# Cross attention with image prompts: inner products by way of DRAM, and two changes of order

## The chip, the cores and the metric

The kernel runs on one core of a Trainium2 chip. Its engines work side by side: TensorE (PE) multiplies, VectorE (DVE), ScalarE (ACT) and GpSimd (POOL) work on elements, SyncE (SP) issues most transfers. The metric is the device time of one execution in microseconds; every number of times below is in that unit.

## The reference

Eight images (B = 8) of 112 query rows and 320 channels attend to 375 context tokens of 512 features, of which the last 4 are image prompts, with 20 heads of 16 channels. What is computed for each image, cut to what matters:

```python
q   = heads(x @ W_q)                       # 20 heads, 112 x 16
k_t = heads(text @ W_k); v_t = heads(text @ W_v)        # text: 371 tokens
probs_t  = softmax(q k_t^T * scale)        # 112 x 371 for each head
text_out = probs_t @ v_t
k_ip, v_ip = heads(ip @ W_k_ip), heads(ip @ W_v_ip)     # ip: 4 tokens
qsem = l2norm(probs_t @ text)              # 112 x 512 for each head
sem  = qsem @ l2norm(ip)^T
fused    = q k_ip^T * scale + 0.5 * sem
probs_ip = softmax(fused) * spatial_mask
out = (text_out + probs_ip @ v_ip) @ W_out + b_out + x
```

## The kernel before

The kernel never forms `probs_t @ text` (512 wide). For its norm it uses the inner products of the tokens with each other (the Gram matrix, 371 x 371, made once for an image): the norm squared of a row of probabilities p is the sum over p G p. Since G is symmetric, only the part from the diagonal on is kept, doubled, the diagonal blocks halved. The product of p with G, with the prompts, with a column of ones and with the values of the head is one chain of matrix products.

**Steps.** The 20 heads of an image are done in 5 groups of 4 heads, so there are 40 steps, written (image, group). A step has these parts:

- *scores* (L797 to L804): one matrix product for each head, 112 x 375.
- *probabilities* (L806 to L821): the maximum on DVE (L810), the exponential on ACT (L814), and a transfer that writes the head's 112 x 371 probabilities p into the buffer xg (L821, issued by SP). xg has two buffers, used by turns.
- *turning* (`transposed`, L823 to L836): DVE turns xg into xgT, twelve blocks of 32 tokens (BLK = 12), in one instruction of twelve blocks or two of six.
- *placing* (`placed`, L759): POOL copies the head group's 16 value columns from vr into the free columns of u (L763), in three pieces.
- *products* (`product`, L843 to L860): twelve blocks times four heads; the four heads sit on four groups of 32 rows of PE. Weights are xgT, the moving operand is u: 392 columns for block 0, 32 fewer with each block.
- *sums* (`reduced`, L907, on DVE; `value_sums`, L881, on ACT).

**The tile u** holds an image's products and value columns once for each of the four row groups of PE: 128 partitions, four quarters of GW = 792 columns. `gram` (L530) makes the products in the tile ug (128 x 792, one buffer), ACT and POOL double and halve them, and `gram_to_groups` (L551) copies quarter q, that is 32 rows of ug, into all four groups of 32 rows of u: four transfers for a quarter. Quarters are copied at different times: for an odd image in the course of the even image before it, after group 1 (quarter 0), after group 2 (quarter 1), a little later (quarter 2, in `behind`) and after group 3 (quarter 3); for an even image after groups 0, 1, a little later, and 3. Value columns go from the tile vext to DRAM (vd, `values_to_dram`, L692) and from there to vr (`values_to_groups`, L712).

**The order** of PE, SP and DVE is written out by hand (later that of ACT and POOL too), and each engine does its instructions in that order. SP's transfers are issued one after another: one that has to wait holds up all behind it. The steps go in pairs: `pair(n)` does steps n and n + 1 and works on the scores and probabilities of steps n + 2 and n + 3 between their products; `moved` is called after each step's products and issues the copies above; `behind(n)` does the projections, products and turnings between the pairs. The first steps, `alone(0)` and what leads to them, are written out from L1206 on.

One transfer has an unusual count of rows: `load_ctx` loads the last 371 - 11 x 32 = 19 rows of the text with four transfers of 19 rows (L146).

Of the kernel before, what the change touches and what calls it, by code (L numbers as in the profile page):

```python
# [8 lines left out]
F32 = mybir.dt.float32  # L9
# [11 lines left out]
def kernel(  # L21
# [14 lines left out]
    nc = tc.nc  # L36
    P = 128
# [13 lines left out]
    RG = 32  # L51
# [9 lines left out]
    GROUP = 4  # L61
    NG = H // GROUP
    BLK = TP // RG
# [3 lines left out]
    GW = GCOL[NT]  # L67
# [16 lines left out]
    dram = ctx.enter_context(tc.tile_pool(name="dram", bufs=2, space=bass.MemoryType.DRAM))  # L84
# [142 lines left out]
    ug = const.tile([P, GCOL[NT]], F32, tag="ug", name="ug")  # L227
# [191 lines left out]
    st = {}  # L419
# [110 lines left out]
    def gram(b):  # L530
# [3 lines left out]
        for c in range(NT):  # L534
# [13 lines left out]
            doubled(ps, c, c, DEAL[c] if left_out(b, c) else ())  # L548
            yield

    def gram_to_groups(b, blocks, eng=nc.sync):  # L551

        for q in blocks:
            for a in range(GROUP):
                eng.dma_start(
                    st[b]["u"][a * RG : (a + 1) * RG, q * GW : (q + 1) * GW],
                    ug[q * RG : (q + 1) * RG, :],
                )
# [153 lines left out]
    def values_to_groups(b, c0=0, c1=NT):  # L712
        s = st[b]
        w = NG * D
        for a in range(GROUP):
            nc.sync.dma_start(
                s["vr"][a * RG : (a + 1) * RG, c0 * QN : c1 * QN].rearrange(
                    "p j g d -> p j (g d)"
                ),
                s["vd"][c0 * P : c1 * P, a * w : (a + 1) * w].rearrange("(j i) x -> i j x", i=RG),  # L720
            )
# [63 lines left out]
    def scores(b, g, a, early=False, ps=None):  # L785
        s = st[b]
        _, qm, j = queries[b]
        i, r = g // 2, g % 2
        if early and (g + a // 2) % 2:

            ps = ps_qd.tile([P, 512], F32, tag="qd", name=f"ps_s_{b}_{g}_{a}")
        elif ps is None:
            ps = ps_sc.tile([P, 512], F32, tag="sc", name=f"ps_s_{b}_{g}_{a}")
        w = T if b > 0 else TT
        if i == FULL:
            r = a // 2
        nc.tensor.matmul(  # L797
            ps[:S, :w],
            qm[a * RG : (a + 1) * RG, i, r, j * S : (j + 1) * S],
            s["kT"][a * RG : (a + 1) * RG, i, :w],  # L800
            start=True,
            stop=True,
        )
        s["sc", g, a] = ps  # L804

    def probabilities(b, g, a):  # L806
        s = st[b]
        ps = s.pop(("sc", g, a))
        nmx = small.tile([S, 1], F32, tag="nmx", name=f"nmx_{b}_{g}_{a}", bufs=8)
        nc.vector.tensor_reduce(nmx, ps[:S, :TT], AX.X, ALU.max, negate=True)  # L810
        if ("p", g) not in s:
            s["p", g] = work.tile([S, GROUP, TT], F32, tag="p", name=f"p_{b}_{g}", bufs=4)
        p = s["p", g][:, a, :]
        nc.scalar.activation(p, ps[:S, :TT], AF.Exp, bias=nmx)  # L814
        if b > 0:
            nc.scalar.copy(s["ipl"][:, groups[g][a], :], ps[:S, TT:T])  # L816

        xg = x_ring[(b * NG + g) % NX]
        rows = xg[a * RG : a * RG + S // QN, :, :TT]
        eng = nc.scalar if (b, g, a) == (B - 1, NG - 1, GROUP - 1) else nc.sync  # L820
        eng.dma_start(rows, p)  # L821

    def transposed(b, g, j0=0, j1=BLK):  # L823

        xg = x_ring[(b * NG + g) % NX]
        if j1 < j0 + 1:
            return
        if ("xT", g) not in st[b]:
            st[b]["xT", g] = work.tile([P, BLK, P], F32, tag="xgT", name=f"xgT_{b}_{g}")
        xT = st[b]["xT", g]  # L830
        n = BLK // (2 if b == B - 1 or (b, g) == (0, 0) or j1 - j0 < BLK else 1)
        for j in range(j0, j1, n):
            nc.vector.transpose(  # L833
                xT[:, j : j + n].rearrange("p j (k q) -> p q j k", q=QN),
                xg[:, :, j * RG : (j + n) * RG].rearrange("p q (j k) -> p q j k", k=RG),
            )  # L836
# [66 lines left out]
    def reduced(b, g, a0=0, a1=GROUP):  # L903
        s = st[b]
        for a, (h, ps) in list(enumerate(zip(groups[g], s["qd", g])))[a0:a1]:
            p = s["p", g][:, a, :]
            nc.vector.tensor_tensor_reduce(  # L907
                out=p,
                in0=ps[:S, :TT],
                in1=p,  # L910
                scale=1.0,
                scalar=0.0,
                op0=ALU.mult,
                op1=ALU.add,
                accum_out=s["ss"][:, h : h + 1],
            )
        if a1 == GROUP:
            del s["p", g]
# [276 lines left out]
    steps = [(b, g) for b in range(B) for g in range(NG)]  # L1195
# [3 lines left out]
    def run(key, make, pieces=1):  # L1199

        if key not in gens:
            gens[key] = make()
        for _ in range(pieces):
            next(gens[key], None)
# [27 lines left out]
    run(("q", 0), lambda: project_queries(pairs[0]))  # L1232
    run(("k", 0), lambda: keys(0))
    run(("q", 0), None)
    values_to_groups(0)
    for a in range(GROUP):
        scores(0, 0, a, early=True)
        probabilities(0, 0, a)
    run(("q", 0), None)
    run(("k", 0), None)  # L1240
    for a in range(GROUP):
# [63 lines left out]
    inputs = {5: (0, 2), 9: (2, 5), 19: (5, B)}  # L1305

    late = (1, 5)

    def pair(n):

        one, two = steps[n], steps[n + 1]
        b, g = one
        tags = ("mm", "sc") if b % 2 and g == NG - 1 else ("sc", "mm")
        ends = (BLK - 2, BLK - 1)

        products_in(b, g, ("qd",) * GROUP)
        for j in range(BLK - 2):
            product(b, g, j, range(GROUP))
            if j < 2:
                heads = (HIGH, LOW)[j]  # L1320
                coming_scores(n + LEAD, heads, tags[j])
                coming_probabilities(n + LEAD, heads)
            if j == 1:
                if n in late:
                    transposed(*two, 0, BLK // 2)
                transposed(*two, BLK // 2, BLK)
            if j % QN == QN - 1:
                placed(*two, (j // QN,))
        if n == 3:
            load_channels(nc.gpsimd, wo_sb, w_out)  # L1330
            nc.gpsimd.dma_start(sm_sb, smask.unsqueeze(1))
            nc.gpsimd.dma_start(bias_sb, b_out.partition_broadcast(S))
        if n in inputs:
            load_inputs(*inputs[n])
        products_in(*two, (tags[1],) * 2 + (tags[0],) * 2)
        for there, here in ((HIGH, LOW), (LOW, HIGH)):
            product(*two, 0, there)
            for j in ends:
                product(b, g, j, here)
        del st[b]["xT", g]  # L1340
        placed(*two, (NT - 1,))
        moved(b, g)
        if g > 1 and g != 2:
            turned(b + 2)
        if b % 2 and g in (0, NG - 1):
            f(b - 1 - (g == 0))
        if g in (1, 2):
            f(b - 1, 2)
        reduced(b, g)
        if g == 2:  # L1350
            turned(b + 2)
        value_sums(b, g)
        if b % 2 == 0 and b > 0 and g == 1:
            turned_inputs(pairs[b // 2 + 1], 0, FULL)

        b, g = two
        for j in range(1, BLK - 2):
            product(b, g, j, range(GROUP))
            if j == 4:
                coming_scores(n + 1 + LEAD, HIGH, "qd")  # L1360
                coming_probabilities(n + 1 + LEAD, HIGH)
            if j == 7:
                coming_scores(n + 1 + LEAD, LOW, "qd")
                coming_probabilities(n + 1 + LEAD, LOW)
        for heads in (HIGH, LOW):
            for j in ends:
                product(b, g, j, heads)
        del st[b]["xT", g]
        moved(b, g)
        if one in ((b, 2), (b, 3)):  # L1370
            turned(b + 2, 1 + (one == (0, 3)))

    def moved(b, g):

        nb = b + 1
        if b % 2 == 0:
            if g in (1, 2):
                gram_to_groups(nb, (g - 1,))
            if g == 3:
                todo = [lambda: gram_to_groups(nb, (3,)), lambda: values_to_groups(nb)]  # L1380
                for move in reversed(todo) if nb == B - 1 else todo:
                    move()
        else:
            if g in (0, 1):
                gram_to_groups(nb, (g,))
            if g == 2:
                values_to_groups(nb, 0, 2)

    def behind(n):

        b, g = steps[n]
        nb = b + 1
        two = steps[n + 1 : min(n + 3, len(steps) - NG + 1)]

        def tr(i):
            if i < len(two):
                transposed(*two[i], 0, BLK // (1 + i))

        if b % 2 == 0 and g == 0:
            if n == 0:  # L1400
# [107 lines left out]
    for n in range(0, len(steps) - NG, 2):  # L1508
# [4 lines left out]
        b, g = steps[n]  # L1513
# [16 lines left out]
    b = B - 1  # L1530
# [18 lines left out]
    for g in range(NG):  # L1549
# [36 lines left out]
        n = (3, 3, 2, 0)[g]  # L1586
# [71 lines left out]
```

## Time and profile before

| | |
|---|---|
| runs of the kernel | 403.81, 405.58, 406.58; median 405.58 |
| the profiled execution | 403.29, of which the span of the profile is 401.6 |
| granted clock of PE | 0.999 |
| transfers, all queues | 65.86 MB, mean 164 GB/s |
| queue of SP and its like (q1), POOL's queue (q0) | 57.7% and 6.0% of 16 engines' time |
| u<-ug on SP | 120 issues of 99.0 KB, median 590 ns each |
| xg<-p on SP | 159 issues of 162.3 KB |
| SP waiting for ACT ahead of xg<-p (L821 <- ACT ipl) | 56.2 in 44 waits |

How to read it: the page's first part gives the busy time of each engine and its share of the span. The chain that ended last is followed back from the last instruction; an engine's share of it says how much of the span that engine set. A row of waits has the engine, what it wanted to do, whom it waited for, the total, the count and the longest wait. A row of the timeline has the start, the length, the engine, the line, the operation with its output and inputs, the count of merged instructions and in square brackets the idle time before it and what ended it. A row of the windows has, for each engine, busy time and count of instructions in that stretch, then the granted clock, the mean busy share of 16 DMA engines and GB/s.

### The profile page before, as it was taken

How to read it: one execution, taken by the hardware profiler on the slowest of the kernel's cores; microseconds unless marked ns; L12 is line 12 of the kernel's file. 1: busy time of each engine (PE TensorE's matmuls, PEld its weight loads, DVE VectorE, ACT ScalarE, POOL GpSimd, SP SyncE). 2: the span in 40 equal slices, each digit the busy share in tenths (PEclk: the TensorE clock that was granted, in tenths of full speed). 3: DMA queues.
4: the chain of work that ended last, by engine and by line, in shares of the span. 5: the costliest groups of instructions: out<-in, count | busy, mean ns of one | idle time of the engine just before them, and what ended most of it. 6: DMA issues, size and time to landing. Idle time of an engine off the chain costs nothing.

```text
span 401.6 us, 14442 instructions
## 1 busy us (share of the span) xinstructions
PE 396.1 (99%) x5685; PEld 320.2 (80%) x5685; DVE 332.2 (83%) x712; ACT 200.2 (50%) x716; POOL 192.5 (48%) x409
## 2 busy tenths in 40 slices
PE   8999999999999999999999999999999999999996
PEld 8768697888878788878787878877887878887894
DVE  4357689877989988987999898897798988888995
ACT  3255343347434853425652665334843485446864
POOL 8655427052562567051573348432256155804781
PEclk9999999999999999999999999999999999999999
DMA  8979657988577846668657766576846544775321
GB/s 239 217 202 258 155 153 178 210 193 190 149 186 155 202 122 187 155 146 184 169 148 167 193 155 169 160 185 140 191 120 175 130 125 116 197 176 166 108 59 29
DMA packets 58119, 65.86 MB, mean 164 GB/s; under 512 B 20165, under 2 KB 51257, under 8 KB 58052
## 3 DMA queue, kind: packets, MB, share of 16 engines
q1 hardware_dynamic: 54814, 58.23, 57.7%
q0 software_dynamic: 2544, 5.92, 6.0%
q8 instruction: 45, 0.74, 0.9%
q10 hardware_dynamic: 694, 0.80, 0.6%
q14 instruction: 22, 0.18, 0.2%
HBM read 20.22 MB, written 5.22 MB: 63 GB/s over the span
## 4 chain that ended last, share of the span: by engine, by line
PE 96%; DVE 2%; ACT 1%; issue 0%; DVEq 0%
PE ps_qd L854 47%; PE ps_k L571 10%; PE ps_g L541 8%; PE ps_s L797 6%; PE ps_v L613 6%; PE ps_vs L671 6%; PE ps_k L588 3%; PE ps_q L402 3%; PE ps_o L1050 2%; PE ps_g L503 1%; DVE xgT L833 1%; PE ps_w L489 1%; PE ps_c L472 1%; PE ps_q L384 1%; PE ps_a L1041 0%
## 5 line engine op out<-in xcount | busy, mean ns | idle before, releaser
L854 PE MATMUL ps_qd<-u,xgT 32*112 32x72 f32 (+10 forms) x3806 | 216.0, 352 | 0.8 <-DVE xgT L833 0.7
L854 PEld LDWEIGHTS ps_qd<-u,xgT 32*112 32x112 f32 x3806 | 177.5, 172 | 33.5 <-issue 4.2
L833 DVE STREAM_TRANSPOSE xgT<-xg 128x768 f32<-128x768 f32 (+1 forms) x63 | 123.1, 1973 | 4.3 <-DMA xg<-p 4.1
L814 ACT ACTIVATE p<-ps_s,nmx 112x371 f32<-112x371 f32 x160 | 85.5, 585 | 64.9 <-DVE nmx L810 63.9
L810 DVE TENSOR_REDUCE nmx<-ps_s 112x1 f32<-112x371 f32 x160 | 76.8, 534 | 26.2 <-PE ps_s L797 24.6
L763 POOL COPY u<-vr 128x64 f32<-128x64 f32 x120 | 26.9, 237 | 140.8 <-PE ps_qd L854 76.8
L907 DVE CUSTOM_DVE_ANT_0 p<-ps_qd,p 112x371 f32<-112x371 f32 x148 | 71.6, 540 | 10.0 <-ACT pvs L881 7.4
L797 PE MATMUL ps_s<-kT,qm 32*112 32x375 f32 (+1 forms) x320 | 61.0, 485 | 0.0
L881 ACT COPY pvs<-ps_qd 112x21 f32<-112x21 f32 x148 | 21.3, 200 | 52.5 <-DVE ss L907 49.9
L571 PE MATMUL ps_k<-ctxT,wk_sb 128*128 128x371 f32 x128 | 43.4, 482 | 0.0
L571 PEld LDWEIGHTS ps_k<-ctxT,wk_sb 128*128 128x128 f32 x128 | 23.1, 190 | 12.8 <-issue 0.8
L541 PE MATMUL ps_g<-ctxT 128*32 128x119 f32 (+11 forms) x672 | 32.7, 338 | 0.0
L541 PEld LDWEIGHTS ps_g<-ctxT 128*32 128x32 f32 x672 | 27.7, 109 | 6.1 <-issue 1.2
L797 PEld LDWEIGHTS ps_s<-kT,qm 32*112 32x112 f32 x320 | 27.3, 171 | 6.3 <-POOL vext L675 1.1
L460 DVE STREAM_TRANSPOSE ctxT<-ct 128x512 f32<-128x512 f32 x21 | 22.5, 1081 | 6.7 <-DMA ct<-in_ctx_dram 6.7
L816 ACT COPY ipl<-ps_s 112x4 f32<-112x4 f32 x140 | 24.3, 174 | 0.0
L613 PE MATMUL ps_v<-wv_sb,ctxT 128*128 128x320 f32 x80 | 23.6, 442 | 0.0
L613 PEld LDWEIGHTS ps_v<-wv_sb,ctxT 128*128 128x128 f32 x80 | 14.5, 190 | 5.6
L578 ACT COPY kT<-ps_k 128x371 f32<-128x371 f32 x16 | 7.5, 469 | 22.2 <-PE ps_k L571 22.2
L1029 POOL TENSOR_TENSOR vip<-vip,w 112x1280 f32<-112x1280 f32 (+1 forms) x8 | 17.5, 2182 | 0.2 <-DVE w L1023 0.2
L525 POOL TENSOR_TENSOR ug<-ug,half 128x128 f32<-128x128 f32 (+1 forms) x24 | 10.7, 451 | 14.3 <-ACT ug L524 13.0
L520 ACT ACTIVATE ug<-ps_g 128x279 f32<-128x279 f32 (+5 forms) x24 | 8.0, 333 | 17.5 <-PE ps_g L541 10.8
(189 smaller groups left out, 469.1 us busy)
## 6 DMA issues: line engine op xcount, KB each, us to landing
xg<-p SPq DMA_DIRECT2D x159, 162.3 KB
u<-ug SPq DMA_DIRECT2D x120, 99.0 KB
ct<-in_ctx_dram SPq DMA_DIRECT2D x28, 176.0 KB
vip<-vipd SPq DMA_DIRECT2D x7, 560.0 KB
vr<-vd SPq DMA_DIRECT2D x20, 120.0 KB
out_dram<-ob SPq DMA_DIRECT2D x7, 140.0 KB
vd<-vext POOLq DMA_DIRECT2D x12, 80.0 KB, 3.4
vr<-vd SPq DMA_DIRECT2D x12, 80.0 KB
```

The costliest lines, as they stand in the source:

```text
L541: nc.tensor.matmul(ps[p * RG : (p + 1) * RG, s0 : T - t0], ctxT[:, e, t0 + q * RG : t0 + (q + 1) * RG], ctxT[:, e, t0 + s0 : T], start=(e ...
L571: nc.tensor.matmul(ps[:, :TT], wk_sb[:, e, i * P : (i + 1) * P], s["ctxT"][:, e, :TT], start=(e == 0), stop=(e == NE - 1),)
L613: nc.tensor.matmul(ps[:, :C], ctxT[:, e, c * P : (c + 1) * P], wv_sb[:, e, :], start=(e == 0), stop=(e == NE - 1),)
L671: nc.tensor.matmul(ps[:, :CH], a[:, k], t[:, k], start=(k == 0), stop=(k == 1))
L763: nc.gpsimd.tensor_copy(region(b, c)[:, :, UV - c * P :], s["vr"][:, c * QN : (c + 1) * QN, g, :])
L797: nc.tensor.matmul(ps[:S, :w], qm[a * RG : (a + 1) * RG, i, r, j * S : (j + 1) * S], s["kT"][a * RG : (a + 1) * RG, i, :w], start=True, st ...
L810: nc.vector.tensor_reduce(nmx, ps[:S, :TT], AX.X, ALU.max, negate=True)
L814: nc.scalar.activation(p, ps[:S, :TT], AF.Exp, bias=nmx)
L816: nc.scalar.copy(s["ipl"][:, groups[g][a], :], ps[:S, TT:T])
L833: nc.vector.transpose(xT[:, j : j + n].rearrange("p j (k q) -> p q j k", q=QN), xg[:, :, j * RG : (j + n) * RG].rearrange("p q (j k) -> p ...
L854: nc.tensor.matmul(banks[a][:S, j * RG : UW], xT[a * RG : (a + 1) * RG, j, :S], region(b, c)[a * RG : (a + 1) * RG, p, q * RG :], start=(j ...
L907: nc.vector.tensor_tensor_reduce(out=p, in0=ps[:S, :TT], in1=p, scale=1.0, scalar=0.0, op0=ALU.mult, op1=ALU.add, accum_out=s["ss"][:, h : ...
```

## The change

Three things change.

1. For images 1 to 7 the products go by way of DRAM. A new function writes ug (128 x 792) to a DRAM tile ud; `gram_to_groups` then reads a quarter, 32 rows, four times over with one transfer into all 128 partitions of u. The write stands where quarter 0 was copied, and quarters 0 and 1 are read where quarter 1 was copied. Image 0 keeps its sixteen copies.
2. In the first steps, `values_to_groups(0)` is called after the scores and probabilities of step (0,0) and no longer ahead of them.
3. In `pair(1)`, after the sums of step (0,1), three blocks (BLK // 4) of step (0,3) are turned; `behind(2)` turns the other nine. `transposed` takes the whole stretch in one instruction where it doesn't divide.

```diff
+    def gram_to_dram(b):
+
+        st[b]["ud"] = dram.tile([P, GW], F32, tag="ud", name=f"ud_{b}")
+        nc.sync.dma_start(st[b]["ud"], ug)
+
     def gram_to_groups(b, blocks, eng=nc.sync):
 
         for q in blocks:
+            if b > 0:
+                eng.dma_start(
+                    st[b]["u"][:, q * GW : (q + 1) * GW],
+                    st[b]["ud"][q * RG : (q + 1) * RG].unsqueeze(0).to_broadcast([GROUP, RG, GW]),
+                )
+                continue
             for a in range(GROUP):
                 eng.dma_start(
                     st[b]["u"][a * RG : (a + 1) * RG, q * GW : (q + 1) * GW],
...
         n = BLK // (2 if b == B - 1 or (b, g) == (0, 0) or j1 - j0 < BLK else 1)
+        if (j1 - j0) % n:
+            n = j1 - j0
         for j in range(j0, j1, n):
...
-    values_to_groups(0)
     for a in range(GROUP):
         scores(0, 0, a, early=True)
         probabilities(0, 0, a)
+    values_to_groups(0)
...
+    ahead = (1,)
...
         reduced(b, g)
+        if n in ahead:
+            transposed(*steps[n + 2], 0, BLK // 4)
         if g == 2:
             turned(b + 2)
         value_sums(b, g)
...
         nb = b + 1
         if b % 2 == 0:
-            if g in (1, 2):
-                gram_to_groups(nb, (g - 1,))
+            if g == 1:
+                gram_to_dram(nb)
+            if g == 2:
+                gram_to_groups(nb, (0, 1))
             if g == 3:
                 todo = [lambda: gram_to_groups(nb, (3,)), lambda: values_to_groups(nb)]
...
         else:
-            if g in (0, 1):
-                gram_to_groups(nb, (g,))
+            if g == 0:
+                gram_to_dram(nb)
+            if g == 1:
+                gram_to_groups(nb, (0, 1))
             if g == 2:
                 values_to_groups(nb, 0, 2)
...
         def tr(i):
             if i < len(two):
-                transposed(*two[i], 0, BLK // (1 + i))
+                done = BLK // 4 if n - 1 in ahead and i == 0 else 0
+                transposed(*two[i], done, BLK // (1 + i))
```

## The prediction

> **What bounds the kernel now.** I read the page first, then PE's waits, then the windows of the end, then the order of time around the places that the diff touches.
>
> ```profile
> span 401.6 us, 14442 instructions
> PE 396.1 (99%) x5685; PEld 320.2 (80%) x5685; DVE 332.2 (83%) x712; ACT 200.2 (50%) x716; POOL 192.5 (48%) x409
> PE 96%; DVE 2%; ACT 1%; issue 0%; DVEq 0%
> PE ps_w L489 <- DVE waker L213: 1.1, 1, 1.1
> PE ps_qd L854 <- DVE xgT L833: 0.7, 1, 0.7
> 380.00:402.00 22.00, 18.25 (x298) 15.86 (x290) 16.21 (x50) 12.54 (x49) 11.29 (x19) 0.97 0.16 45
> ```
>
> TensorE (PE) is busy for 396.1 of 401.6 us and is 96% of the chain that ended last. Its idle time is 5.5 us: 1.1 at the start, 3.75 in the last 22 us (22.00 less 18.25), and one stall of 0.7 us ahead of the products (L854). The change adds and removes no PE work. So it can gain that stall and little else; but whatever makes a product wait costs its full length. The question is which transfers have slack.
>
> **The three blocks of one turning.**
>
> ```profile
> 48.37 3.58 SPq L821 DMA_DIRECT2D xg<-p  x4
> 54.76 0.99 DVE L810 TENSOR_REDUCE nmx<-ps_s 112x1 f32<-112x371 f32 x2 [1.01 <-PE ps_s L797]
> 59.48 3.01 DVE L833 STREAM_TRANSPOSE xgT<-xg 128x1536 f32<-128x1536 f32 x1
> 60.65 1.30 PE L402 MATMUL ps_q<-xT,wq_sb 128*128 128x224 f32 x6
> 62.64 0.60 PE L854 MATMUL ps_qd<-u,xgT 32*112 32x392 f32 x4 [0.69 <-DVE xgT L833]
> ```
>
> The stall is here: PE ends its projections at 61.95 and waits until the turning of step (0,3), twelve blocks in 3.01 us, is done. The change puts three of the blocks (3.01 / 4 = 0.75 us) ahead of the maxima at 54.76, where VectorE (DVE) sat idle for 1.01 us. They need the probabilities whose last load SP issued by 48.37 + 3.58 = 51.95. With the 1.9 us from issue to use that a row below shows, they are there at 53.9, the blocks end near 54.6, and the maxima don't move. Nine blocks take 2.26 us, so the turning ends near 61.75, ahead of PE: the stall of 0.69 us goes, and PE's own projections are late next. Bounds: a gain of 0.69, or, if the probabilities come late, a loss of at most the 0.75 by which maxima can be pushed. I take -0.7, as the idle time holds the blocks. The new remainder test in the turning only lets pieces of three and nine blocks be cut; it adds one instruction and changes nothing else.
>
> **The first group's order.**
>
> ```profile
> 23.79 1.87 SPq L716 DMA_DIRECT2D vr<-vd  x4
> 24.41 1.95 ACT L814 ACTIVATE p<-ps_s,nmx 112x371 f32<-112x371 f32 x4 [0.52 <-DVE nmx L810]
> 25.76 7.29 SPq L821 DMA_DIRECT2D xg<-p  x8
> 28.00 0.24 POOL L763 COPY u<-vr 128x64 f32<-128x64 f32 x1 [3.27 <-DMA vr<-vd]
> 34.19 1.22 PE L854 MATMUL ps_qd<-u,xgT 32*112 32x392 f32 x10
> ```
>
> The four loads of value columns move behind the first four writes of probabilities in SP's queue: four times 0.91 us (7.29 / 8), that is 3.65 us less the 0.86 by which the first probabilities can start earlier (25.76 to 24.9, the first of ACT's four at 24.41 plus a quarter of 1.95), so the loads end near 30.4 instead of 25.66. POOL's copy followed the last of them by 2.3 us and would run near 32.7, ahead of the products at 34.19 by 1.5 us. What stands behind it on POOL (input loads, constants, the halving of the next products) slips by 4.7 us and has no reader before 40 us. No idle time stands before the products at 34.19, so the earlier turning gains nothing. I take 0. Bounds: 0, and +0.8 if the loads take twice the 2.3 us.
>
> **Inner products by way of DRAM.** Before, each image's products go to the four row groups of u in sixteen copies of 32 rows (four quarters, four copies each). After, one write puts all 128 rows into DRAM where quarter 0 was copied, quarters 0 and 1 are read together where quarter 1 was copied, and 2 and 3 stay in their places: five issues for sixteen, in images 1 to 7, and 7 x 0.41 = 2.8 MB more to move on 65.86 (page, section 3). A quarter is 128 rows of 3,168 B, 405 KB.
>
> ```profile
> 59.62 5.02 SPq L555 DMA_DIRECT2D u<-ug  x8
> 65.86 3.92 SPq L821 DMA_DIRECT2D xg<-p  x4
> 69.83 2.48 SPq L555 DMA_DIRECT2D u<-ug  x4
> 72.56 3.22 SPq L716 DMA_DIRECT2D vr<-vd  x4
> 82.35 0.93 PE L854 MATMUL ps_qd<-u,xgT 32*112 32x392 f32 x8
> 235.04 1.22 SPq L146 DMA_DIRECT2D ct<-in_ctx_dram  x4
> 38.50:39.50 1.00, 1.00 (x44) 1.00 (x36) 1.00 (x1) 0.00 (x0) 0.24 (x1) 1.00 1.01 404
> 62.00:64.00 2.00, 1.36 (x17) 1.02 (x21) 2.00 (x4) 0.00 (x0) 2.00 (x5) 1.00 0.73 170
> 236.50:237.50 1.00, 1.00 (x24) 0.82 (x20) 1.00 (x3) 1.00 (x5) 0.24 (x1) 1.00 0.07 20
> ```
>
> The write costs what a quarter cost (same bytes, same place), and the wait of the reads for it is covered: it is issued where 52 us stood and read 7 us later. SP gains eleven issues of about 0.6 us an image, but SP isn't what PE waits for. What matters is how fast one read of a quarter runs. In the windows the last two columns are the busy share of sixteen DMA engines and GB/s. While the copies of 32 rows run (62 to 64) nearly all engines work. [...] The new read's source has an outermost count of 4 (the repeated copies) ahead of the 32 rows. No load of before has a count of 4, so no row gives its price; between one engine and all, I expect it to be spread over four.
>
> [...]
>
> The price: from DRAM in long pieces one engine moves 404 / 16 = 25 GB/s (window 38.5), so four move 101 and a quarter takes 4.0 us. At the 20 GB/s of the other window it takes 5.1. Spread over all sixteen it takes no more than the 2.4 us of 170 GB/s. I take 4.3: the 404 row is nearest (reads from DRAM, kilobytes long), and 7% go to POOL's queue and the instruction queues, which share the engines. Three quarters issued together then hold four engines for 12.9 us, and everything that SP issues after them queues behind on those engines.
>
> Image 1: first data 1.3 us after 59.62 (part of the 1.9), the three quarters end at 73.8, the four probability writes (0.6 each) at 76.2, quarter 3 at 80.5, the value columns at about 82.9; landing 0.6 and POOL's copy 0.25 give 83.8 against products that start at 82.35: a stall of 1.4.
>
> ```profile
> 98.23 5.03 SPq L555 DMA_DIRECT2D u<-ug  x8
> 103.65 2.05 SPq L707 DMA_DIRECT2D vd<-vext  x4
> 110.03 1.89 SPq L716 DMA_DIRECT2D vr<-vd  x4
> 112.29 3.53 SPq L821 DMA_DIRECT2D xg<-p  x4
> 117.79 2.49 SPq L555 DMA_DIRECT2D u<-ug  x4
> 122.19 0.41 POOL L763 COPY u<-vr 128x64 f32<-128x64 f32 x2 [4.86 <-DMA u<-ug]
> L854 PE MATMUL ps_qd<-u,xgT 32*112 32x392 f32 x2 | 0.5, 497 | 0.0
> 193.00 5.03 SPq L555 DMA_DIRECT2D u<-ug  x8
> 212.25 2.51 SPq L555 DMA_DIRECT2D u<-ug  x4
> 287.33 5.03 SPq L555 DMA_DIRECT2D u<-ug  x8
> 309.31 2.50 SPq L555 DMA_DIRECT2D u<-ug  x4
> 343.18 5.32 SPq L555 DMA_DIRECT2D u<-ug  x8
> 350.38 4.04 SPq L821 DMA_DIRECT2D xg<-p  x4
> 356.66 2.50 SPq L555 DMA_DIRECT2D u<-ug  x4
> 363.89 0.93 PE L854 MATMUL ps_qd<-u,xgT 32*112 32x392 f32 x8
> ```
>
> Image 2 is tighter, for SP itself waits: the loads of value columns (110.03) may only be issued when the writes of 103.65 have landed, and the next probabilities (112.29) stand behind them. POOL's copy at 122.19 came 1.9 us after the copies' last issue (117.79 + 2.49). After: three quarters end at 98.23 + 1.3 + 12.9 = 112.4, the value writes land at 113.2, SP issues the loads until 115.1, the probabilities until 118.6, the next value writes until 119.8, quarter 3 then; it ends at 119.9 + 1.3 + 4.3 = 125.5 and lands at 126.1, and with POOL's copy the first products of step (2,0), of which the groups by form over 124.36 to 124.5 show two beginning (the row with 392 columns and x2), start at 126.4: a stall of 2.0 against 124.4. Image 4 has the same spacing (193.00 to 212.25 is 19.3 us, as 98.23 to 117.79 is 19.6): 2.0 again. Image 6 has 22.0 us: 0. Image 7: 343.18 + 1.3 + 12.9 = 357.4, probabilities 359.8, value columns 362.2 (this image has them first), quarter 3 at 366.5, and 0.85 more is 367.4 against 363.89: 3.5. Images 3 and 5 start later behind the same order and I give them 0.
>
> **The sum**: 1.4 + 2.0 + 2.0 + 3.5 = 8.9, less 0.7, is +8.2 us. Against the profiled execution (403.29 us, span 401.6) that is 411.5; the median of the runs shown, 405.58, stands 2.3 above the profiled one, and on it the forecast is 413.8. Ends of the unknown price: at 2.4 us a quarter all of it is covered and -0.7 is left (404.9); at 5.1 us each of the images 1, 2, 4 and 7 loses 4 x 0.8 = 3.2 more and images 3, 5, 6 begin to lose too, about +22 (427).
>
> **The rivals.**
>
> *Spread wide.* If the read goes over all engines, transfers end where they ended, SP has fewer issues, and only the 0.7 us of the turning is left: 404.9, not slower. For it: the 32-row copies do use nearly all engines, and the new read also has 128 rows at its destination. Against it: the window of the 19-row loads. It decides from a price of about 3.5 us a quarter downwards, where image 2's quarter 3 lands in time.
>
> [...]
>
> *Four engines, but covered.* With 3.3 to 3.8 us a quarter, stalls are under 1 us at two or three places, and the time is 404.9 to 408. Against it: no window shows an engine above 25 GB/s.
>
> *Four engines, and dearer.* At 5.1 us and more a quarter, probabilities too land after DVE wants them, in every image: 427 or above. For it: the 20 GB/s of the 19-row loads. Against it: those are pieces of 512 B.
>
> *Value columns late in the first group.* +0.8 at most, worked out above; it would be lost in the others.
>
> **How the numbers follow.** Four engines at about 4.3 us a quarter: 0.48, and this is the forecast, 413.8. Dearer: 0.12. Four engines but covered: 0.12. Spread wide: 0.26. Something that gains over 1% has 0.02, since PE idles 5.5 us in all and 4.9 of it lie at the two ends. A measurement of this kernel can tell about 1% (4 us) from no change. So slower by over 1% has 0.48 + 0.12 = 0.60, within 1% 0.12 + 0.26 = 0.38, faster 0.02. The range reaches from 404.0 (the wide spread less the scatter of the runs, which lay from 403.81 to 406.58) to 427 (the dear end); the forecast's own range is 409 to 419.
>
> **What the profile after would show.** Turning right: no idle time before the products after PE's projections near 62, and two turnings of step (0,3), of about 0.75 and 2.3 us. First group: POOL's first copy near 32.7, and no idle time before the products at 34. Four engines: windows just behind the three reads with a DMA share near 0.3 and some 100 GB/s where the copies stood at 0.73 and 170; idle time of PE before L854, put down to POOL's copy, at the first step of images 1, 2, 4 and 7; longer waits of POOL's copy for u. If instead those windows show 170 GB/s or more and PE's waits only lose the 0.7, the spread was wide and the forecast is wrong. If waits of DVE for the probabilities grow to several us in every image, the price was higher than I took.

## The result, and the profile after

Six runs of the changed kernel have a median of 482.15 us (475.21 to 483.19), six of the kernel before 406.37 (403.81 to 410.21): a ratio of 1.178, 95% interval 1.168 to 1.188. A ratio leaves out the runs that lie over 1.5% above the fastest of the same kernel, so it need not be the quotient of the two medians. The change makes the kernel slower by some 75 us. The forecast was +8 us, with a range that ended at 427. The profiled execution after has a span of 475.4 us against 401.6, so the trace shows 73.8 us of it.

From the page after, its span, busy times and chain of waits:

```profile
span 475.4 us, 14318 instructions
PE 415.9 (87%) x5685; PEld 338.0 (71%) x5685; DVE 331.6 (70%) x713; ACT 200.7 (42%) x716; POOL 192.1 (40%) x409
PE 47%; DMA 27%; DVE 4%; SPq 3%; issue 2%; POOL 2%; ACT 1%; POOLq 0%; DVEq 0%
```

TensorE was 96% of the chain and is 47% now; transfers, which had no share, have 27%. TensorE's idle time went from 5.5 to 59.5 us. Its busy time also grew, by 19.8 us for the same 5685 instructions. The waits of TensorE (PE) name the places (us in total, times, longest):

```profile
PE ps_qd L867 <- POOL u L774: 24.0, 3, 10.5
PE ps_g L541 <- POOL ctxT L448: 18.2, 2, 9.7
PE ps_qd L867 <- DVE ctxT L460: 7.6, 2, 3.9
```

The two longest waits of the first row, 10.5 and 10.1 us, stand ahead of the first products of images 1 and 7; the second row's, 9.7 and 8.5 us, stand ahead of inner products and fall in the stretches of images 3 and 5, to which the prediction gave nothing. GpSimd (POOL) is only the last link: it copies value columns into u when they land. The chain between 60 and 100 us, in order of time, shows what held them (start, us, what):

```profile
65.62 19.86 DMA u<-ud
...
86.44 1.36 SPq L727
...
87.85 8.20 DMA vr<-vd
...
96.28 0.25 POOL u L774
...
96.58 2.25 PE ps_qd L867 x10
```

The third read of a quarter of image 1 lands 19.9 us after its issue. Only then do the loads of value columns go out, and they need 8.2 us more. The timeline of SP's queue after, at the same place (start, us, issues):

```profile
64.36 1.78 SPq L560 DMA_DIRECT2D u<-ud  x3
...
69.67 5.61 SPq L832 DMA_DIRECT2D xg<-p  x4
81.27 0.57 SPq L560 DMA_DIRECT2D u<-ud  x1
85.55 3.47 SPq L727 DMA_DIRECT2D vr<-vd  x4
```

Before, quarter 3 was issued at 69.83 and the value columns at 72.56. And the windows after (us, busy times, clock, DMA share, GB/s):

```profile
80.00:85.00 5.00, 5.00 (x66) 3.57 (x69) 1.93 (x8) 1.14 (x4) 0.00 (x0) 1.00 0.26 99
90.00:94.00 4.00, 0.00 (x0) 0.00 (x0) 1.53 (x3) 0.00 (x0) 0.00 (x0) 0.50 0.56 133
98.00:104.00 6.00, 6.00 (x72) 4.74 (x68) 4.16 (x6) 2.29 (x8) 3.32 (x8) 0.64 0.42 102
```

From 80 to 85 us little but a read moves, and the share is 0.26 at 99 GB/s: four of sixteen engines at 25 GB/s each. That step of the prediction holds. In the gap TensorE's granted clock falls to 0.50, and from 98 to 104 us it is 0.64 on average.

A table made from the profiled executions, one of each kernel, is the best guide to where the time went. It takes the starts of the products of each image's second step, (k,1), and gives what each image's stretch took over that of before, in us (the last column is the span). It holds most of the runs that are told of below.

```
                            to (0,1)   1     2     3     4     5     6     7    all
changed kernel                  3.6  13.3   6.6  12.3   8.0  10.2   6.6  13.0  73.8
way by DRAM alone               1.4  11.4   9.5  12.1   9.2  11.7   8.9  12.5  77.0
four transfers a quarter        4.0   0.3   0.0   0.0  -0.5   0.0  -0.5   0.0   3.4
only quarter 1 in one           3.8   3.0   2.4   0.0   1.5   0.0   0.5   1.0  12.8
only quarters 1 and 2 in one    3.7   7.0   2.5   3.1   3.5   5.7   0.4   4.8  30.9
only image 3 in one             0.2   0.9   1.1  11.5  -0.5   0.0  -0.1   0.0  13.7
two transfers a quarter         1.7  28.3  26.4  26.8  25.3  26.8  24.3  27.2 187.0
extra load, GpSimd's queue      0.0   9.1  10.0   7.8   8.6   7.8   8.9   6.8  60.3
extra load, SP's queue          1.9  14.5  11.3  13.9   9.1  12.7   5.6  12.2  82.6
```

Every image from 1 to 7 loses 6.6 to 13.3 us. The prediction had 1.4, 2.0, 0, 2.0, 0, 0, 3.5. The first column scatters from run to run with the loads at the start.

### The profile page after: what moved, and what is told of

It reads as the page before. It is cut to its first block, busy times and chain, and to the rows that moved or that the text cites. A ratio compares the mean times of both kernels' runs of the same rounds, so it can differ in the third digit from the quotient of the medians.

```text
span 475.4 us, 14318 instructions
## 1 busy us (share of the span) xinstructions
PE 415.9 (87%) x5685; PEld 338.0 (71%) x5685; DVE 331.6 (70%) x713; ACT 200.7 (42%) x716; POOL 192.1 (40%) x409
## 4 chain that ended last, share of the span: by engine, by line
PE 47%; DMA 27%; DVE 4%; SPq 3%; issue 2%; POOL 2%; ACT 1%; POOLq 0%; DVEq 0%
PE ps_qd L867 26%; DMA u<-ud 15%; DMA vr<-vd 6%; PE ps_g L541 6%; DMA xg<-p 4%; PE ps_k L582 4%; PE ps_vs L682 3%; PE ps_s L808 3%; PE ps_v L624 2%; DMA vd<-vext 2%; DVE xgT L846 2%; PE ps_k L599 2%; SPq L832 1%; SPq L727 1%; DVE nmx L821 1%
## 5 line engine op out<-in xcount | busy, mean ns | idle before, releaser
L867 PE MATMUL ps_qd<-u,xgT 32*112 32x72 f32 (+9 forms) x3806 | 227.8, 365 | 36.0 <-POOL u L774 24.0
L867 PEld LDWEIGHTS ps_qd<-u,xgT 32*112 32x112 f32 x3806 | 189.0, 178 | 69.1 <-POOL u L774 33.3
L846 DVE STREAM_TRANSPOSE xgT<-xg 128x768 f32<-128x768 f32 (+2 forms) x64 | 122.1, 1926 | 47.9 <-DMA xg<-p 46.3
L821 DVE TENSOR_REDUCE nmx<-ps_s 112x1 f32<-112x371 f32 x160 | 76.7, 532 | 47.7 <-PE ps_s L808 46.3
L808 PE MATMUL ps_s<-kT,qm 32*112 32x375 f32 (+1 forms) x320 | 63.6, 503 | 0.0
L541 PE MATMUL ps_g<-ctxT 128*32 128x119 f32 (+11 forms) x672 | 36.8, 366 | 18.2 <-POOL ctxT L448 18.2
L541 PEld LDWEIGHTS ps_g<-ctxT 128*32 128x32 f32 x672 | 30.5, 115 | 25.8 <-POOL ctxT L448 19.2
L808 PEld LDWEIGHTS ps_s<-kT,qm 32*112 32x112 f32 x320 | 28.8, 178 | 6.3 <-issue 1.4
L582 PEld LDWEIGHTS ps_k<-ctxT,wk_sb 128*128 128x128 f32 x128 | 23.1, 190 | 12.8 <-issue 0.8
```

Source lines behind the costliest of these rows:

```text
L541: nc.tensor.matmul(ps[p * RG : (p + 1) * RG, s0 : T - t0], ctxT[:, e, t0 + q * RG : t0 + (q + 1) * RG], ctxT[:, e, t0 + s0 : T], start=(e ...
L582: nc.tensor.matmul(ps[:, :TT], wk_sb[:, e, i * P : (i + 1) * P], s["ctxT"][:, e, :TT], start=(e == 0), stop=(e == NE - 1),)
L808: nc.tensor.matmul(ps[:S, :w], qm[a * RG : (a + 1) * RG, i, r, j * S : (j + 1) * S], s["kT"][a * RG : (a + 1) * RG, i, :w], start=True, st ...
L846: nc.vector.transpose(xT[:, j : j + n].rearrange("p j (k q) -> p q j k", q=QN), xg[:, :, j * RG : (j + n) * RG].rearrange("p q (j k) -> p ...
L867: nc.tensor.matmul(banks[a][:S, j * RG : UW], xT[a * RG : (a + 1) * RG, j, :S], region(b, c)[a * RG : (a + 1) * RG, p, q * RG :], start=(j ...
```

## The experiments

**The three parts alone.** Each of the first three kernels makes one part of the change; their diffs are parts of the diff above. Every ratio is against runs of the kernel before made beside that kernel; their medians lay from 405.53 to 406.40 us.

> Only the first group's order is changed (probabilities of the first step ahead of the loads of its value columns); products by 16 copies and whole turnings as before. Theory (reads held to four DMA engines, SP standing still behind them, TensorE clocked down after idling, all from the way by DRAM): within 1% of before, 405.5 to 409, since in the changed kernel the products of the first step began only just behind POOL's copy (37.8 against 37.5). Rival (the first group's order costs several us by itself, as the whole start of the changed kernel lies 3.4 us later): 409 or more.

Measured: 404.77 us against 405.53, ratio 1.001 (0.997 to 1.004). The timelines of ScalarE (ACT), SP, GpSimd and TensorE in this run show that it is a near thing:

```profile
25.80 1.95 ACT L814 ACTIVATE p<-ps_s,nmx 112x371 f32<-112x371 f32 x4 [0.52 <-DVE nmx L810]
...
30.12 2.08 SPq L716 DMA_DIRECT2D vr<-vd  x4
...
35.41 0.67 POOL L763 COPY u<-vr 128x64 f32<-128x64 f32 x3 [12.49 <-DMA xg<-p]
...
35.70 1.22 PE L854 MATMUL ps_qd<-u,xgT 32*112 32x392 f32 x10
```

The products start 0.29 us behind the first of GpSimd's copies, and no idle time of TensorE's stands before them. From ScalarE's first probabilities to the first product it is 35.70 - 25.80 = 9.9 us, before 34.19 - 24.41 = 9.8. The order costs nothing, with almost nothing to spare; that the first products of the changed kernel start 3.6 us later (37.80) isn't the order either: it had these probabilities at 27.89, and another kernel with the same order (the 64 products below) at 25.21, so the start scatters from run to run.

> Only the three blocks of one turning are put ahead of the maxima. Theory: 0.7 us less than before (the idle time of PE ahead of the products at 62.64 goes), at most 1.0; no stall anywhere else. Rival (the blocks wait for the probabilities' load and push the maxima behind them): no gain, up to 0.8 us more.

Measured: 405.76 us, ratio 1.000 (0.997 to 1.004). The timelines of VectorE (DVE) and TensorE in this run:

```profile
56.69 0.88 DVE L835 STREAM_TRANSPOSE xgT<-xg 128x384 f32<-128x384 f32 x1 [1.02 <-issue]
57.42 1.82 DVE L810 TENSOR_REDUCE nmx<-ps_s 112x1 f32<-112x371 f32 x4
...
61.85 2.31 DVE L835 STREAM_TRANSPOSE xgT<-xg 128x1152 f32<-128x1152 f32 x1
...
64.15 1.28 PE L856 MATMUL ps_qd<-u,xgT 32*112 32x392 f32 x10
```

The stall ahead of these products is gone: their row has no idle time. From step (0,2) to (0,3) it is 11.5 us in place of 11.9. But the idle time of 1.02 us still stands ahead of the three blocks. They wait in it and then push the maxima, which start 57.42 - 54.76 = 2.7 us later in a run that is 1.9 us later here (50.31 against 48.37 for the same issue). The gain is 0.4 us and isn't seen in the whole. In the changed kernel, which has all three parts, even this is missing: the same stretch takes 11.95 us against 11.91, since TensorE now waits for probabilities (p) that the pushed maxima make late, a wait that the kernel before doesn't have. From TensorE's waits after:

```profile
PE ps_kipT L331 <- ACT p L825: 0.5, 1, 0.5
```

> Only the products' way by DRAM. Theory: nearly all of the loss, 470 to 490. Rival (the loss comes from the three edits together, with the later start and the cut turning opening the first gap): under 460.

Measured: 479.86 us, ratio 1.188 (1.181 to 1.195). The whole loss lies in the way by DRAM.

**The spread of the reads.** The changed kernel with each quarter read by four transfers:

```diff
-                eng.dma_start(
-                    st[b]["u"][:, q * GW : (q + 1) * GW],
-                    st[b]["ud"][q * RG : (q + 1) * RG].unsqueeze(0).to_broadcast([GROUP, RG, GW]),
-                )
+                for a in range(GROUP):
+                    eng.dma_start(
+                        st[b]["u"][a * RG : (a + 1) * RG, q * GW : (q + 1) * GW],
+                        st[b]["ud"][q * RG : (q + 1) * RG],
+                    )
```

> The changed kernel, with each quarter read from DRAM by four transfers of 32 rows in place of one transfer that repeats 32 rows four times: same bytes, same places in the program, more issues. Theory (four engines are the cause): the reads spread as the copies of before did, and nearly all of the loss goes: 404 to 414. Rival 1 (the write and the read by DRAM are slow in themselves, whatever the spread): 460 or more. Rival 2 (quarter 0 read 7 us later and together with quarter 1 is what makes the burst): 425 to 460, with PE's waits at the first steps of images 1, 3, 5 and 7. If the number of issues mattered, it would be slower than the changed kernel, as it has 12 more an image.

Measured: 405.9 us, ratio 1.002 (0.999 to 1.005). The same bytes go the same way through DRAM, at the same places and with more issues, and nothing is lost. So neither DRAM, nor the order of the reads, nor the number of issues is the cause; it is the form of the transfer: one in four repeated copies, or four of 32 rows.

Two transfers of two copies each (`for a in (0, 2)`, with `to_broadcast([2, RG, GW])`):

> The changed kernel with each quarter read by two transfers of two copies. Theory (a transfer whose outermost count is the number of copies goes to so many engines, the same ones each time): two engines carry everything, some 8 us a quarter, and the loss about doubles, 540 to 600. If the two transfers go to different pairs of engines: as the changed kernel, 470 to 490. Rival (the repeated source as such is slow, with any count): 470 to 490 too, with the DMA share at 0.25 as before and not at 0.13.

Measured: 590.33 us, ratio 1.454 (1.445 to 1.463). A window of this run in which only reads move:

```profile
92.00:94.00 2.00, 0.00 (x0) 0.00 (x0) 0.00 (x0) 0.00 (x0) 0.00 (x0) 0.50 0.13 50
```

The share is 0.13, two of sixteen, at 25 GB/s each. The trace's packets say it once more. For each run, the time in us in which exactly so many packets of the quarter's size were under way at once:

```
packets at once                      1      2     3      4     5..16 (most of any)
changed kernel (3,168 B)          13.4   20.9  15.8  104.7   13.7
two transfers a quarter (3,168 B) 31.6  235.3  15.1    1.1    1.6
before (3,168 B)                  14.3    5.2   3.4    3.3   10.1 (at 15)
```

**How many, and in which image.** The first two kernels use the four transfers except for quarter 1 (`if q == 1`), then for quarters 1 and 2 (`if q in (1, 2)`); the third except for image 3 (`if b == 3`).

> Every quarter is read by four transfers of 32 rows, except quarter 1 of each image, which is one transfer of four copies. Theory (the price of one quarter, 4 to 5 us, was right, and it is the queue of three that hurts): one alone is covered, 404 to 410. Rival (any transfer on four engines makes SP stop long enough to be seen): 412 to 430.

Measured: 416.47 us, ratio 1.020 (1.009 to 1.031). One quarter alone isn't covered: the time lies in the rival's range.

> As the kernel with quarter 1 alone, but quarters 1 and 2 are each one transfer of four copies, issued one behind the other. Theory (SP stands still once eight later transfers stand behind a read that has not landed): two quarters take 8 to 10 us, a part of the loss, 408 to 430. By the sum of the prediction, with queues alone, two quarters are covered everywhere: 404 to 408. If the loss is by number of quarters, half of it: 440.

Measured: 434.86 us, ratio 1.070 (1.063 to 1.077), between the theory's 430 at most and the 440 of a loss by number of quarters. Over images 1 to 7 the table has 8.4 us for one quarter, 27.0 for two and 70.0 for all four: the loss grows faster than the number.

> All quarters by four transfers of 32 rows, except image 3's, which are one transfer of four copies each. Theory (each image loses by itself; steps (2,4) to (3,0) were 12.3 us longer in the changed kernel): 416 to 420, and all steps from (3,1) on as long as in the kernel with four transfers. The prediction gave image 3 nothing: 404 to 407.

Measured: 417.25 us, ratio 1.027 (1.022 to 1.033). Image 3 loses 11.5 us and the images behind it nothing. TensorE's largest wait in this run is the one that the changed kernel has there, and GpSimd's timeline shows what stands behind it:

```profile
PE ps_g L541 <- POOL ctxT L448: 9.2, 1, 9.2
```

```profile
183.99 0.59 POOL L781 COPY u<-vr 128x64 f32<-128x64 f32 x3 [18.38 <-DMA vr<-vd]
184.52 0.20 POOL L448 COPY ctxT<-ipnT 128x16 f32<-128x16 f32 x1
```

GpSimd stands 18.38 us at its copy of the value columns, and the short copy that TensorE's inner products need comes behind it in GpSimd's order.

**SP's standing still, or the engines.** SP's transfers tell of their landing by semaphores (counters). In the trace after, SP's 351 issue records carry eight of them by turns, and 131 of the records name the one that they carry themselves as what they wait for, that is the landing of an earlier transfer. So in the changed kernel SP waits for landings of reads that it doesn't need yet, 16.1 us ahead of probabilities (L832) and 14.3 ahead of loads of value columns (L727). SP's waits after:

```profile
SPq L832 <- DMA u<-ud: 16.1, 8, 4.6
...
SPq L727 <- DMA u<-ud: 14.3, 5, 4.0
```

My theory was that this makes most of the loss. The next two kernels give the reads to another queue (`nc.scalar.dma_start`, then `nc.gpsimd.dma_start`).

> The changed kernel, with the reads of a quarter (still one transfer that repeats 32 rows four times) issued by ScalarE instead of SP. [...] Theory (most of the loss comes from SP, which stops issuing probabilities and value columns until the reads have landed): SP goes on, and more than half of the loss goes, 410 to 440; SP's waits for the reads' landings are gone from the waits of its queue. Rival (what SP issues is held up on the four engines themselves, where it queues behind the reads): 455 or more, with the loads issued early and landing late.

Measured: 476.95 us, ratio 1.162 (1.152 to 1.172). It tells nothing apart, since SP's waits after show the same transfers, though ScalarE issues them now:

```profile
SPq L832 <- DMA u<-ud: 20.7, 8, 4.1
...
SPq L727 <- DMA u<-ud: 19.8, 4, 6.3
```

> The changed kernel with the quarter reads issued through GpSimd's queue. In the run with ScalarE, SP still waited for the reads' landings, so that run didn't separate the two. If GpSimd's transfers end on events of their own, SP no longer waits for them. Theory (SP's standing still makes most of the loss): 410 to 440, if the transfer is still on four engines. Rival (what SP issues queues behind the reads on the four engines): 455 or more with the DMA share near 0.26 while only reads run. If GpSimd's queue spreads a transfer over all engines, the share is 0.5 or more and the time 405 to 415, which would say only that the spread belongs to the queue.

Measured: 464.34 us, ratio 1.135 (1.125 to 1.144). SP's waits for reads are gone from the view, and most of the loss stays. SP's and GpSimd's timelines in this run, and one of GpSimd's waits:

```profile
80.83 1.92 SPq L727 DMA_DIRECT2D vr<-vd  x4
...
94.01 0.64 POOL L774 COPY u<-vr 128x64 f32<-128x64 f32 x3 [4.96 <-DMA vr<-vd]
```

```profile
POOL u L560 <- DMA ud<-ug: 25.5, 4, 9.9
```

The value columns are issued by 82.75 and used at 94.01, 11.3 us later; in the first group before it was 2.3 us. They are issued in time and land late: by the trace's events, a read that GpSimd issued at 80.73 landed at 91.77, and three of the four loads that SP issued right behind it, from 81.24 on, landed from 92.11 to 93.91. But GpSimd now waits itself, and 25.5 us of it for the write into DRAM, so the last three kernels load the engines with transfers that nobody reads. To the kernel with four transfers they add, at each quarter:

```diff
+                flat = ehs.rearrange("n t e -> (n t e)")
+                extra = dram.tile([GROUP, RG, GW], F32, tag=f"x_{b}_{q}", name=f"x_{b}_{q}", bufs=1)
+                nc.gpsimd.dma_start(extra, flat[: RG * GW].rearrange("(r w) -> r w", w=GW).unsqueeze(0).to_broadcast([GROUP, RG, GW]))
```

with `nc.sync` in the second, and `flat[: P * GW]` as 128 different rows in the third.

> The kernel with four transfers of 32 rows a quarter (no loss), and beside each quarter one extra transfer of the same 405 KB in four repeated copies, from an input in DRAM to a place in DRAM that nobody reads, issued through GpSimd's queue. Nothing waits for its landing. Theory 1 (four engines are held, and every transfer of SP that has a share on them lands late): most of the loss comes back, 440 to 490. Theory 2 (the loss needs SP to stand still, or a reader that waits for the quarter itself): 404 to 415.

Measured: 463.45 us, ratio 1.137 (1.129 to 1.145).

> As the kernel with the extra transfers on GpSimd's queue, but SP issues them, so that SP's later issues also wait for their landings. Theory 1: no more than 20 us over the kernel with GpSimd's queue. Theory 2: 450 or more while the other stays under 415.

Measured: 485.75 us, ratio 1.198 (1.190 to 1.207). SP's waits in this run (x is the extra transfer's place):

```profile
SPq L561 <- DMA x<-in_ctx_dram: 23.5, 10, 3.2
SPq L836 <- DMA x<-in_ctx_dram: 17.9, 11, 2.9
```

> The control: extra transfers of the same bytes on GpSimd's queue, but of 128 different rows (no repeated copy), so spread over all engines. Both theories: under 412. If the extra 11 MB as such cost the time, it is as slow as the four-copy one.

Measured: 429.45 us, ratio 1.054 (1.047 to 1.062), more than both theories gave: the extra 11 MB cost 23 us by themselves, so the transfers seem to have little slack. The same bytes in four repeated copies cost 34 us more (463.45 - 429.45), though SP waits for none of these landings and nobody reads them. What lands late are some of SP's own transfers: VectorE's waits for the probabilities' landing are 3.8 us in the kernel with four transfers, 20.8 with the extra load of 128 rows and 36.8 with the one in four copies (longest 1.7, 3.0 and 6.9). SP stands a little longer behind its own probabilities too, 12.8 us ahead of the reads against 8.9 in the control. I put the 34 us down to the held engines, on which parts of SP's transfers would stand behind the extra ones; that is an explanation, and no trace here gives a transfer's parts by engine. The packets differ as well, 50,688 B in the four copies and 25,344 B in the 128 rows (3,168 B in the changed kernel), and no run takes this apart. Issued by SP the transfers cost another 22 us, just over the 20 that the first theory allowed. My theory, that SP's standing still makes most of the loss, falls: in these kernels it is the smaller part.

Nor need all of that smaller part be SP's. The packets of the extra transfers (50,688 B) ran four at once for 101.3 us when SP issued them, and more than four for 0.3 us; on GpSimd's queue eight ran at once for 15.6 us and twelve for 4.1. It would fit these counts that SP's all use the same four engines and GpSimd's different ones, but the packets' records don't name the engine. What SP's waits cost and what it cost that SP's hardly ever ran more than four at once was not told apart.

**The clock.** The changed kernel with work on constants in TensorE's idle time: ahead of the first products of image 1 and of the inner products of images 4 and 6.

```diff
+    def warm(ps, n):
+
+        for _ in range(n):
+            nc.tensor.matmul(ps[:, :P], waker, waker, start=True, stop=True)
...
+            if b in (4, 6) and c == 0:
+                warm(ps, 40)
...
+        if one == (1, 0):
+            warm(st[b]["qd", g][0], 44)
```

The first try had 64 products at each place; its condition for image 7 met no step, so that gap stayed empty.

> The changed kernel with 64 products on constants (about 8 us of TensorE at full clock, results not used) where TensorE stands idle for about 10 us: ahead of the first products of images 1 and 7 and of the inner products of images 4 and 6. Theory (the clock falls because TensorE idles, and costs about 20 us in all, two thirds of it behind these four gaps): the extra work costs nothing and 10 to 14 us go, 464 to 472; the granted clock stays near 1.0 behind these gaps. Rival (the clock isn't set by idling, or the slow work lies beside other waits): no gain or more time, 478 to 490.

Measured: 484.82 us, ratio 1.193 (1.184 to 1.202). The 64 products took 14.6 us, longer than the gap, so it decides nothing; the 8 us reckoned for them were my estimate, and no row shows them.

> As the kernel with work on constants put into TensorE's idle time, but less of it: one such product took 0.22 us, not 0.13, and 64 of them 14.3 us, more than the gap they were to fill. Now 44 (9.9 us) ahead of image 1's first products and 40 (9.0 us) ahead of the inner products of images 4 and 6. Theory (the clock falls through idling, and each fall costs 2 to 2.6 us behind its gap): step (1,0) to (1,1) falls from 7.8 to 5.1 us at a start of (1,0) that is no later, and 4 to 6 us of the whole go. Rival (step (1,0) is long because later parts of the products arrive late, not because of the clock): it stays at 7 us or more.

Measured: 474.92 us, ratio 1.170 (1.164 to 1.176): against 1.178 (1.168 to 1.188) no difference that can be told. TensorE's timeline in this run:

```profile
84.78 10.09 PE L517 MATMUL ps_qd<-waker 128*128 128x128 f32 x88
94.90 1.22 PE L874 MATMUL ps_qd<-u,xgT 32*112 32x392 f32 x10
...
138.01 2.25 PE L874 MATMUL ps_qd<-u,xgT 32*112 32x392 f32 x10 [5.66 <-DVE xgT L853]
```

Where the gap is filled (44 products, two records each) the ten products behind it take 1.22 us, as before; behind the gap left at 138.01 they take 2.25. The granted clock is 1.00 from 95 to 100 us; in the changed kernel it is 0.60 from 96 to 104. From (1,0) to (1,1) it is 5.1 us, in the changed kernel 7.8. So the gap of 10.5 us lowered the clock, as theory said. But in this trace the time is given back: the stretch that ends in image 2 is longer by as much (steps (1,3) to (1,4) took 18.6 us against 13.7). The transfers seem to set the pace, and the 19.8 us of slower products seem to lie for the most part in time that would be waited anyway.

**The harmless parts together**: three blocks, four transfers a quarter, the first group's order as before.

> The parts that cost nothing together: the three blocks of one turning, the way by DRAM with four transfers of 32 rows a quarter, and the first group's order as before. By the steps of the runs so far the order costs 0.9 us at the first products, the blocks gain 0.4 and the way by DRAM gains 0.5 in each of images 4 and 6: 404 to 406, at most 0.4% under before, which is less than such runs tell apart. Rival (the steps' differences are given back at the end): 405.5 to 407.

Measured: 404.57 us, ratio 0.996 (0.993 to 0.999): 0.4% under before, the only kernel here whose interval lies under it, and too little to be called faster. The 0.9 us that the expectation gives the order was misread: it was counted from the first write of probabilities, which the order itself puts earlier. From ScalarE's first probabilities there is none.

## Why the prediction failed

**The bound: right.** TensorE had 5.5 us of idle time, no part of the change could gain more, and what makes a product wait costs its full length.

**Three blocks, -0.7: the stall went, the gain mostly not.** The blocks found no idle time: their data came when that was over, and they pushed the maxima by some 0.7 us, the bound that the prediction named for a loss. With this part alone TensorE waited for neither, and the stretch was 0.4 us shorter. In the changed kernel TensorE waited 0.5 us for probabilities behind the pushed maxima, and no gain was left.

**First group's order, 0: right, with less slack than claimed.** The loads' issue was to end at 30.4 with GpSimd's copy at 32.7. In the run with this part alone, which is 1.4 us later at this place (25.80 against 24.41), they came at 32.2 and 35.4: the issue as reckoned to 0.4 us, the landing a full microsecond later. Of the 1.5 us to spare 0.3 was left.

**Four engines: right.** No row of before shows a transfer of four repeated copies; that it would be spread over four was my estimate, between the shares of 0.07 (loads of 19 rows) and 0.73 (copies of 32). The runs showed 0.26 at 99 GB/s for four copies and 0.13 at 50 for two; other counts were not tried. The rivals with a wide spread and with covered reads are out. The price was right as a pace: in images 2, 4 and 6 the second of three reads landed 3.9 to 4.3 us behind the first, against 4.3 predicted. In images 1, 3, 5 and 7, where more ran beside the reads, it was 6.2 to 9.1.

**The dearer rival.** It had a chance of 0.12, and 482 us lies in its region, 427 or above. Its sign came true too: VectorE's waits for the probabilities' landing grew from 4.1 us in all to 46.3, and in each of images 1 to 7 one took 3.0 to 8.0 us. Yet its reason, an engine at 20 GB/s, did not: four engines moved 99 GB/s, and a packet of 3,168 B took 126 ns, that is 25 GB/s an engine. So this sign doesn't tell a dear price from a queue behind the reads.

**The stalls, 8.9 us: the step that failed.** Three things in it were wrong.

- "First data 1.3 us after" the issue and 4.3 to the end made 5.6, or 6.2 with the landing. The 1.3 held: by the traces' packets the first one started 1.29 us behind the issue at 59.62 before, 1.39 behind the one at 64.36 after. But a first read landed 7.2 to 8.6 us after its issue, and three of them took 16.6 to 21.1 us in place of 14.2, or 14.8 with the landing. The 7% put on for what shares the engines was too little. In image 1 the three reads were 6.3 us longer than reckoned (64.36 to 85.48, that is 21.1), and the wait was 10.5 us in place of 1.4.
- "Images 3 and 5 start later behind the same order and I give them 0": no working stood behind it. Image 3 by itself costs 11.5 us. With image 6 these three are 29 of the 70 us in the table.
- The sum let each transfer queue behind the reads once, and stopped there. What SP issued beside the reads landed late: writes of values from SP's queue took 9.7 us from issue to landing after (median, by the events in the trace) against 2.4 before, loads of value columns for images 1 to 7 took 4.7 against 2.7, and up to 14.4. What waits for these comes late in turn, and SP waited for landings itself. "SP isn't what PE waits for" was true before and not after.

The range's dear end was reckoned from the price of a quarter alone, 5.1 us, with the stalls worked out in the same way. By the prediction's sum no price in the rows would have reached 482; the waits behind the reads did.

## What to carry to other kernels

Look at the form of a transfer before its bytes: one in four repeated copies ran on four engines (a share of 0.26, 99 GB/s), and four transfers of 32 rows that move the same bytes cost nothing (405.9 against 482 us). Price such a transfer not by its own length but by all that is issued beside it and behind it, and work out a stall for every place where it stands, those that seem to have time too. Where a kernel is 99% bound by one engine, a queue that comes under pressure can cost more than ten times what the engine had to gain (here some 75 us against 5.5).

## What the runs showed of the hardware

- A short gap can be enough for the clock. With one quarter in one transfer, TensorE's timeline and the windows behind it:

```profile
87.64 1.40 PE L874 MATMUL ps_qd<-u,xgT 32*112 32x392 f32 x10 [1.91 <-POOL u L781]
```

```profile
88.00:90.00 2.00, 2.00 (x20) 2.00 (x18) 0.12 (x1) 0.00 (x0) 1.92 (x3) 0.64 0.76 193
90.00:92.00 2.00, 2.00 (x20) 2.00 (x16) 1.51 (x4) 1.20 (x5) 2.00 (x6) 0.51 1.12 223
92.00:94.00 2.00, 2.00 (x47) 2.00 (x45) 2.00 (x3) 1.09 (x4) 0.39 (x3) 1.00 0.28 59
```

  After 1.91 us of waiting the granted clock is 0.64 and 0.51 in these two windows, and the stretch from (1,0) to (1,1) takes 6.7 us in place of 5.1. Not every such gap does: over all profiled executions, the two ends left out, a clock of 0.50 followed 16 of the 37 gaps of 1.2 to 3.1 us, and all of the 59 longer ones.
- Reads issued by ScalarE didn't free SP: it waited 40.5 us for their landings (20.7 + 19.8).
- The transfers of this kernel have little room: 11 MB more, in sixteen packets of 25,344 B a transfer, cost 23 us (429.45 against 406.31 before).
